# Attention in seven products: reordering the key loads, a third score half, the first denominators and the tail statistics

## The chip, the cores and the metric

The kernel runs on one core of one Trainium2 chip. The metric is the device time of one launch in microseconds, as the median of several runs. All times below are in microseconds unless they say otherwise. PE is TensorE's matmul row, PEld its weight loads, DVE is VectorE, ACT is ScalarE, POOL is GpSimd and SP is SyncE.

## What is computed

The input is four images of 256 channels and 64 x 64 positions, in fp32. The first layer is attention over all 4096 positions; the second is a block of cluster attention, an MLP and a pointwise convolution. Cut to what matters:

```
q = wq x + bq;  k = wk x + bk;  v = wv x + bv        # 32, 32 and 256 channels
attn = softmax(q^T k over all 4096 keys)
x = gamma * (v attn^T) + x                           # layer 0
y = x + ls1 * cluster(group_norm(x))                 # layer 1
y = y + ls2 * (W2 gelu(W1 group_norm(y)))
out = relu(bn(Wp relu(bn(y * dw))))
```

The group norm of layer 1 needs mean and variance over a whole image, so it can only begin when the attention of that image is complete.

## The kernel before

**Units.** `attention` (from L318) handles one image ("batch"). Its 4096 queries are eight blocks of 512 (`nb`), its keys eight groups of 512 (`g`). A unit `u = 8 nb + g` is one query block against one key group; there are 64 a batch. The 512 x 512 weights of a unit times the 512 x 256 values are done as a two by two block product with seven products in place of eight: `exps` (L591) subtracts the maxima (two L597 on DVE) and takes exponentials (L601 to L603 on ACT), `factors` (L608) makes the sums of quarters (L620 on DVE, four L606 on POOL), and `weigh` (L658) issues the 28 matmuls (L676) in four parts, 0 to 3, each part one or two of the seven products.

**Scores ahead of their use.** Scores are made up to eleven units ahead (`LEAD`), in halves: `half(u, h)` (L465) issues two matmuls of keys against queries (`products`, L433), ACT copies the result from PSUM into one of twelve slots (`kept`, L446), and DVE takes the elementwise maximum into `top` (L457). The two-buffer PSUM pool for scores has one buffer taken by the maxima (`hold`), so each half waits until the half before it has been released. Normally the release comes from DVE's maximum, which reads PSUM; a half marked `kept_only` is released by ACT's copy alone, and its maximum goes on the list `held`, to be taken from the slot later by `caught(n)`, in order of entry. The table `at` (from L865) spreads the halves over the units: two in a normal unit, ahead of parts 0 and 2 (`due`), and three, ahead of parts 0, 1 and 3, in the units listed in `three`, where they are `kept_only`.

**What else runs in a unit.** `weighting` (L888) writes the order of all engines by hand; `manual_schedule` keeps it, and each engine executes its own instructions in that order. In the order of a block:

- `begun(u)` (L413), with the first half of a unit, issues the load of the next unit's keys (`k_unit`, L411, 256 KB, on SP's queue; two key buffers).
- At `g = 1` and 2 of every block but the first, `total` (L724) reduces the block before to its denominators: DVE transposes and reduces (L544, L545), ACT copies (L551), DVE reduces again, takes the reciprocal (L735) and transposes (L561), then `rows` calls `everywhere` (L96), which writes a row of 512 values to DRAM (L99) and reads it back into all partitions (L100), both on SP's queue. The tile `few` that these steps write in is set to zero on POOL at its first use in a batch (L539).
- At `g = 5`, `highest` (L564) does the same for the maxima of the next block; `known` (L580, ACT) puts them into `hold` at `g = 6`. In block 0, transposes on PE do this instead (`short`).
- `gather` (L684) adds the partial denominators at `g = 7` (L692), on POOL, and on DVE in the last block.
- `evict` (ACT, L706) and `combined` (POOL, L717 to L722) turn the seven products' banks into the block's output; `leave` (POOL, L746) multiplies by the reciprocals and `sent` (two DMAs on SP's queue, L754) stores it.
- In the last units `tail` loads the input again (L106), adds the stored attention to it by DMA on POOL's queue (`back`, L770, and `back_one`, L775), and loads the weights that follow. `pooled` (L797) and `seen` (L792), both DVE, take cell sums and normalisation statistics of query blocks 0 to 5, one block per unit, as the table `views` says: units 57 to 62.

After unit 63 the last denominators are summed on PE (L1011) and inverted (L1020), the last block is finished on DVE (L721, L722, L1036, L788), its statistics are taken, and `group_norm` begins (L287, L289). PE is given filler meanwhile (`fill`): the value projection of the next batch (L388), or in batch 3 the last block of batch 2's MLP, which `mlp` leaves over for `late_block` (L1409). Its `begin` is called in unit 61 of batch 3: per channel half a copy of y on POOL (L1419) and a scaling on ACT (L1420), then a subtraction on POOL (L1429). `turn_mlp` (L230) forms two weight combinations on POOL (L233, L234), in batch 3 in the last `tail`.

Of the kernel before, what the change touches and what calls it, by code (L numbers as in the profile page):

```python
# [11 lines left out]
ALU = mybir.AluOpType  # L12
AX = mybir.AxisListType

P = 128
B, C, H, W = 4, 256, 64, 64
# [5 lines left out]
D = 32  # L22
# [38 lines left out]
def attention_then_cluster_block(  # L61
# [34 lines left out]
    def everywhere(dst, rows, name):  # L96

        d = dram.tile([NB], F32, tag="row", name=f"row_{name}")
        nc.sync.dma_start(out=d.rearrange("(a b) -> a b", b=D), in_=rows)  # L99
        nc.sync.dma_start(out=dst, in_=d.partition_broadcast(P))  # L100

    def load_x(b, t, dma=nc.sync):
        xb = x[b].rearrange("(k p) h w -> p k (h w)", p=P)
# [175 lines left out]
    def table(f):  # L279

        nc.scalar.activation(probe, probe, f)
# [36 lines left out]
    def attention(b, xs, ys):  # L318
# [240 lines left out]
        def rows(one, low, dst, name):  # L559

            nc.vector.transpose(low[:D, :D], one)  # L561
            everywhere(dst, low[:16, :D], name)

        def highest(nb):  # L564

            fold(nb)
            top = tops.pop(nb)
            low = spare()[:, nb % 2]
            steps = reduced(top[:, 0], top[:, 1], low, ALU.max, nc.scalar.copy)
            next(steps)  # L570
            yield
            next(steps)
            yield
            one = next(steps)
            mb = work.tile([P, NB], F32, tag="w2", bufs=1, name=f"mr_{b}_{nb}")
            rows(one, low, mb, f"mx_{b}_{nb}")
            yield mb

        def known(mb):
            nc.scalar.copy(own["hold"][:, 0], mb)  # L580
# [143 lines left out]
        def total(nb):  # L724

            few = spare()
            low = few[:, 2]
            flipped = few[:, 3:].rearrange("p a n -> p (a n)")
            steps = reduced(rdens[nb], flipped, low, ALU.add, nc.scalar.copy)
            next(steps)  # L730
            yield
            next(steps)
            yield
            one = next(steps)
            nc.vector.reciprocal(one[:, :16], one[:, :16])  # L735
            rows(one, low, rdens[nb], f"rd_{b}_{nb}")
            yield

        def over(nb):
# [127 lines left out]

        todo = [(p, h) for p in range(GRP + 1, units) for h in range(2)]
        for u in range(units):
            three = u in (1, 3, 9, 11)  # L870
            for part in (0, 1, 3) if three else (0, 2) if u else (1, 3):
                if todo:
                    p, h = todo.pop(0)
                    assert p <= u + LEAD
                    at[u, part] = p, h, three or not u
# [12 lines left out]
        def weighting(next_x, fill, early, begin):  # L888

            mb, av, den, peak, quarters = None, None, iter(()), iter(()), iter(())  # L890

            views = {units - 7 + i: i for i in range(6)}
            shifts = {units - 10: 0, units - 9: 1, units - 8: 2, units - 7: 3}

            def tail(u):


                for at_u, f in (
                    (units - 12, lambda: load(0)),
                    (units - 11, lambda: load(1)),  # L900
                    (units - 10, lambda: (load(2), back(0))),
                    (units - 9, lambda: (load(3), back(1))),
                    (units - 8, lambda: back(2)),
                    (units - 5, lambda: (next_x(), next_x())),
                    (units - 4, lambda: (load_mix(b), next_x())),
                    (units - 4, lambda: b == B - 1 and load_mlp(b)),
                    (units - 3, lambda: (next_x(), begin())),
                    (units - 2, lambda: b < B - 1 and load_mlp(b)),
                    (units - 1, lambda: b == B - 1 and turn_mlp()),
                ):  # L910
                    if u == at_u:
                        f()

            for u in range(units):
# [10 lines left out]
                        )  # L925
                    ]
                maxima = due(u, 0)
                if g == GRP - 1:
                    gather(nb)
                if g + 1 < GRP or more:  # L930
                    exps(u + 1)
# [2 lines left out]
                if nb < 2 or g == 6:  # L934
                    caught(1)

                if nb and g == 1:
                    den = total(nb - 1)
                    next(den)
                elif nb and g == 2:  # L940
                    next(den)
                elif ripe:
                    peak = highest(nb + 1)
                    next(peak)
                if early and nb > 1:
                    early.pop(0)()
                if u in views:
                    pooled(views[u])
                    seen(views[u], (0,))
                weigh(u, av, 0)  # L950
                if short:
                    two = ps_s.tile([P, 2, NB], F32, tag="s", name=f"tt_{b}_{nb + 1}")
# [29 lines left out]
                    spread(nb + 1, dgs["dg"])  # L982
                for f in due(u, 3):
                    f()
                if nb and g == 1:
                    next(den)
                elif nb and g == (4 if more else 3):
                    leave(nb - 1)
                elif nb and g == (5 if more else 4):
                    sent(nb - 1)  # L990
                weigh(u, av, 3)
                if g == 3 and nb + 2 < NBLK:
                    q_block(nb + 2)
# [10 lines left out]
            nb = NBLK - 1  # L1004
            for _ in range(4):
                next(quarters)
            table(AF.Sqrt)
            two = ps_s.tile([P, 2, NB], F32, tag="s", name=f"den_{b}_{nb}")
            den, inv = two[:, 0], two[:, 1]
# [399 lines left out]
    def late_block(b, y, gab):  # L1409
# [5 lines left out]
        def begin():  # L1415
            held["x"] = spool.tile([P, 2, KC, NB], F32, tag="s", name=f"xl_{b}")
            held["y"] = spool.tile([P, 2, KC, NB], F32, tag="s", name=f"yl_{b}")
            for k in range(KC):
                nc.gpsimd.tensor_copy(held["y"][:, 0, k], y[k])  # L1419
                nc.scalar.activation(  # L1420
                    held["x"][:, 0, k],
                    y[k],
# [3 lines left out]
                )  # L1426

            x = held["x"]
            nc.gpsimd.tensor_tensor(x[:, 1, 0], x[:, 0, 0], x[:, 0, 1], ALU.subtract)  # L1429

        def hidden(j):
            return held["h", j // 4][:, j % 4]
# [617 lines left out]
```

## Time and profile before

| | us |
|---|---|
| median of 3 runs (lowest to highest) | 3172.92 (3171.77 to 3178.33) |
| the profiled execution, its own time | 3181.04 |
| its span, first to last instruction | 3179.1 |
| PE busy, share | 3063.0, 96% |
| DVE busy, share | 2508.3, 79% |
| POOL busy, share | 2315.7, 73% |
| ACT busy, share | 1778.2, 56% |
| mean granted PE clock | 0.991 |

The 64 units of the four batches begin at 74.4, 860.4, 1637.9 and 2389.9 and end at 542.8, 1318.4, 2096.0 and 2860.5. In a line of the timeline the columns are start, duration, engine, line, operation, output and inputs with shapes, and in brackets how long the engine stood idle before it and what ended that. SPq is SP's instruction queue. In a line of waits the three numbers are the total, how often, and the longest. The profiler infers who ended a wait; matmul ends are modelled.

### The profile page before, as it was taken

The page shows a single profiled execution, that of the slowest core. Times are in us where ns is not written, and L with a number is a line of the kernel's source. Part 1 is how long each engine was busy: PE and PEld are TensorE (multiplying, and loading weights), DVE is VectorE, ACT ScalarE, POOL GpSimd, SP SyncE. Part 2 cuts the span into 40 slices and gives each one's busy share as a digit, 9 for nine tenths or more (in the row PEclk, how much of TensorE's full clock was granted, in tenths as well). Part 3 has the DMA queues.
Part 4 walks back from the last instruction along what each step waited for, and adds up shares of the span by engine and source line. Part 5 has one row for each costly group of instructions (what it writes and reads, how often), then busy time and mean ns, then how long its engine had stood idle before and what let it go on. Part 6 is the DMA issues. An engine that isn't in the chain of part 4 may idle for free.

```text
span 3179.1 us, 41316 instructions
## 1 busy us (share of the span) xinstructions
PE 3063.0 (96%) x14210; PEld 2503.5 (79%) x14210; DVE 2508.3 (79%) x3573; ACT 1778.2 (56%) x2815; POOL 2315.7 (73%) x2219
## 2 busy tenths in 40 slices
PE   7999999999999999999999999999999999998999
PEld 5777888788678888878867888886877788875786
DVE  3888888677788888877778888877768888876675
ACT  4656664545556666454455666644546566654444
POOL 3888888378578888647758888955767887893663
PEclk9999999999999999999999999999999999999999
DMA  5121126100111223510011212431011112150000
GB/s 165 40 63 60 54 64 190 67 20 27 46 48 59 61 62 98 153 57 27 18 57 44 67 60 64 119 128 44 27 40 50 57 50 67 54 151 1 14 21 27
DMA packets 105873, 200.39 MB, mean 63 GB/s; under 512 B 14416, under 2 KB 30400, under 8 KB 104128
## 3 DMA queue, kind: packets, MB, share of 16 engines
q1 hardware_dynamic: 101856, 181.94, 18.1%
q0 software_dynamic: 2976, 14.70, 2.4%
q8 instruction: 113, 1.85, 0.2%
q10 hardware_dynamic: 832, 1.11, 0.1%
q14 instruction: 96, 0.79, 0.1%
HBM read 149.37 MB, written 48.34 MB: 62 GB/s over the span
## 4 chain that ended last, share of the span: by engine, by line
PE 65%; POOL 13%; DVE 10%; DMA 5%; issue 3%; ACT 3%; SPq 0%; POOLq 0%; ACTq 0%; DVEq 0%
PE av L676 27%; PE mo L1662 9%; PE sc L433 6%; PE hq L1745 5%; POOL acc L606 4%; DMA k<-k 3%; PE hp L1745 3%; PE hr L1745 3%; PE fv L1234 3%; POOL t L606 3%; DVE top L457 2%; POOL s L606 2%; PE vp L388 2%; DVE s L597 2%; PE mo L1646 1%
## 5 line engine op out<-in xcount | busy, mean ns | idle before, releaser
L446 ACT COPY s<-sc 128x1024 f32<-128x1024 f32 x512 | 515.4, 1012 | 466.6 <-PE sc L433 455.4
L597 DVE TENSOR_TENSOR s<-s,hold 128x1024 f32<-128x1024 f32 x512 | 598.3, 1208 | 7.0 <-ACT hold L580 4.2
L606 POOL TENSOR_TENSOR acc<-acc,t 128x512 f32<-128x512 f32 x408 | 541.3, 1347 | 0.0
L606 POOL TENSOR_TENSOR s<-t,s 128x512 f32<-128x512 f32 x256 | 346.2, 1353 | 263.8 <-DVE t L620 197.0
L676 PE MATMUL av<-t,v 128*128 128x256 f32 x2048 | 530.3, 381 | 4.5 <-DVE t L620 2.4
L676 PE MATMUL av<-s,sum 128*128 128x256 f32 x2048 | 526.4, 379 | 4.5 <-POOL s L606 4.3
L676 PE MATMUL av<-s,v 128*128 128x256 f32 x2048 | 528.3, 381 | 2.1 <-ACT xn L1613 1.1
L457 DVE TENSOR_TENSOR top<-sc,top 128x1024 f32<-128x1024 f32 x350 | 426.6, 1219 | 47.1 <-ACT s L446 43.0
L620 DVE TENSOR_TENSOR t<-s,hold 128x1024 f32<-128x1024 f32 x256 | 311.3, 1216 | 191.4 <-POOL acc L606 82.2
L433 PE MATMUL sc<-q,k 128*128 128x512 f32 x1024 | 395.3, 471 | 58.5 <-DMA k<-k 27.0
L676 PEld LDWEIGHTS av<-t,v 128*128 128x128 f32 x2048 | 388.5, 191 | 69.2 <-DVE t L620 8.9
L676 PEld LDWEIGHTS av<-s,v 128*128 128x128 f32 x2048 | 389.1, 190 | 65.3 <-ACT xn L1613 2.3
L676 PEld LDWEIGHTS av<-s,sum 128*128 128x128 f32 x2048 | 388.4, 190 | 60.3 <-POOL s L606 7.6
L1700 ACT ACTIVATE hs<-hs,pv_s 128x256 f32<-128x256 f32 x496 | 232.7, 503 | 352.3 <-DVE hs L1736 352.3
L1662 PE MATMUL mo<-hs,w 128*128 128x256 f32 x1512 | 384.8, 381 | 0.0
L606 POOL TENSOR_TENSOR t<-s 128x512 f32<-128x512 f32 x256 | 329.7, 1288 | 54.5 <-PE av L676 41.2
L1662 PEld LDWEIGHTS mo<-hs,w 128*128 128x128 f32 x1512 | 283.8, 190 | 46.9 <-ACT hs L1700 6.2
L433 PEld LDWEIGHTS sc<-q,k 128*128 128x128 f32 x1024 | 175.6, 191 | 148.9 <-DVE top L457 68.4
L601 ACT ACTIVATE hold<-s 128x512 f32<-128x512 f32 x256 | 154.2, 602 | 224.4 <-DVE s L597 224.0
L603 ACT ACTIVATE s<-s 128x1024 f32<-128x1024 f32 x256 | 266.9, 1042 | 0.0
L1736 DVE TENSOR_TENSOR hs<-hq,hs 128x256 f32<-128x256 f32 x496 | 198.3, 420 | 86.0 <-PE hq L1745 76.0
L676 PE MATMUL av<-t,sum 128*128 128x256 f32 x1024 | 262.4, 378 | 0.0
(292 smaller groups left out, 4856.0 us busy)
## 6 DMA issues: line engine op xcount, KB each, us to landing
k<-k SPq DMA_DIRECT2D x256, 256.0 KB, 2.7
x<-in_x SPq DMA_DIRECT2D x62, 512.0 KB, 6.6
out<-xn SPq DMA_DIRECT2D x62, 256.0 KB, 2.1
att<-t SPq DMA_DIRECT2D x56, 256.0 KB, 3.8
x<-att POOLq DMA_DIRECT2D x12, 1024.0 KB, 9.7
q<-q SPq DMA_DIRECT2D x32, 256.0 KB, 4.1
w<-in_w SPq DMA_DIRECT2D x8, 1024.0 KB, 11.5
k<-hl_k SPq DMA_DIRECT2D x28, 256.0 KB, 2.6
```

The lines of the kernel that those rows point to most:

```text
L433: nc.tensor.matmul(sc[:, r, :], k_s[:, (2 * h + r) * P : (2 * h + r + 1) * P], qs[u // GRP], start=True, stop=True,)
L446: nc.scalar.copy(slots[u][:, PAIR[h]].rearrange("p h r n -> p r h n"), tiles(sc))
L457: nc.vector.tensor_tensor(top, src, top if saved[nb] is None else saved[nb], ALU.max)
L597: nc.vector.tensor_tensor(sh, sh, mb.to_broadcast([P, 2, 2, QW]), ALU.subtract)
L603: nc.scalar.activation(s[:, PAIR[1]], s[:, PAIR[1]], AF.Exp)
L606: nc.gpsimd.tensor_tensor(out, x, y, op)
L620: nc.vector.tensor_tensor(t31[u], s[:, B11 : B22 + 1 : 2], b12.to_broadcast([P, 2, 2, QW]), ALU.add)
L676: nc.tensor.matmul(av[bank][:, half_ * QW : (half_ + 1) * QW], a[:, r], t[:, r], start=(g == 0 and r == 0 and i in (1, 7, 2, 4)), stop=(g ...
L1662: return nc.tensor.matmul(bank[:, half * HB : (half + 1) * HB], a[:, j], t, start=start, stop=stop)
L1700: nc.scalar.activation(src, src, AF.Gelu_apprx_tanh, bias=pvc("b1", P, j + 4 * (i > 1)))
L1736: nc.vector.tensor_tensor(dst, ps, term, ALU.add)
L1745: nc.tensor.matmul(out, w, x, start=True, stop=True)
```

## The change

Seven edits, all in the order of work:

1. `everywhere` returns the reading of the row as a function instead of issuing it. `total` calls it at once. `highest` yields once more: the reading (L100) is issued at the beginning of `g = 6`, behind that unit's first half and so behind its key load, and `sent` of the block before follows it there (before, at the end of `g = 5`).
2. The units with three halves are 1, 3, 7 and 9 instead of 1, 3, 9 and 11.
3. In block 1, `total` begins at `g = 2` instead of `g = 1` and ends at `g = 3`.
4. A unit with three halves calls `caught(1)` once more, ahead of part 3.
5. `views` is a unit later (units 58 to 63), and `gather` of the last block comes behind that unit's first statistics instead of ahead of them.
6. `turn_mlp` in batch 3 comes behind the first four steps of the last `combined` instead of ahead of them.
7. In `late_block.begin`, the copies go from POOL to ACT and the subtraction from POOL to DVE.

```diff
         nc.sync.dma_start(out=d.rearrange("(a b) -> a b", b=D), in_=rows)
-        nc.sync.dma_start(out=dst, in_=d.partition_broadcast(P))
+        return lambda: nc.sync.dma_start(out=dst, in_=d.partition_broadcast(P))
...
             nc.vector.transpose(low[:D, :D], one)
-            everywhere(dst, low[:16, :D], name)
+            return everywhere(dst, low[:16, :D], name)
...
-            rows(one, low, mb, f"mx_{b}_{nb}")
+            fetch = rows(one, low, mb, f"mx_{b}_{nb}")
             yield mb
+            fetch()
+            yield
...
-            rows(one, low, rdens[nb], f"rd_{b}_{nb}")
+            rows(one, low, rdens[nb], f"rd_{b}_{nb}")()
...
-            three = u in (1, 3, 9, 11)
+            three = u in (1, 3, 7, 9)
...
-            views = {units - 7 + i: i for i in range(6)}
+            views = {units - 6 + i: i for i in range(6)}
...
-                    (units - 1, lambda: b == B - 1 and turn_mlp()),
...
                 maxima = due(u, 0)
-                if g == GRP - 1:
+                if more and nb and g == GRP - 2:
+                    next(peak)
+                    sent(nb - 1)
+                if g == GRP - 1 and more:
                     gather(nb)
...
-                if nb and g == 1:
+                when = 1 if nb > 1 else 2
+                if nb and g == when:
                     den = total(nb - 1)
                     next(den)
-                elif nb and g == 2:
+                elif nb and g == when + 1:
                     next(den)
...
                     seen(views[u], (0,))
+                if g == GRP - 1 and not more:
+                    gather(nb)
                 weigh(u, av, 0)
...
-                if nb and g == 1:
+                if nb and g == when:
                     next(den)
                 elif nb and g == (4 if more else 3):
                     leave(nb - 1)
-                elif nb and g == (5 if more else 4):
+                elif nb and g == 4 and not more:
                     sent(nb - 1)
+                if (u, 0) in at and (u, 1) in at:
+                    caught(1)
                 weigh(u, av, 3)
...
             for _ in range(4):
                 next(quarters)
+            if b == B - 1:
+                turn_mlp()
...
-                nc.gpsimd.tensor_copy(held["y"][:, 0, k], y[k])
+                nc.scalar.copy(held["y"][:, 0, k], y[k])
...
-            nc.gpsimd.tensor_tensor(x[:, 1, 0], x[:, 0, 0], x[:, 0, 1], ALU.subtract)
+            nc.vector.tensor_tensor(x[:, 1, 0], x[:, 0, 0], x[:, 0, 1], ALU.subtract)
```

## The prediction

> **What bounds the kernel now.** I read the page's engine line and its chain first.
>
> ```profile
> PE 3063.0 (96%) x14210; PEld 2503.5 (79%) x14210; DVE 2508.3 (79%) x3573; ACT 1778.2 (56%) x2815; POOL 2315.7 (73%) x2219
> ...
> PE 65%; POOL 13%; DVE 10%; DMA 5%; issue 3%; ACT 3%; SPq 0%; POOLq 0%; ACTq 0%; DVEq 0%
> ```
>
> TensorE (PE) sets the time; an edit pays only where PE stands still. Next, busy time by stretch: query blocks 1, 2 and 7 of batch 1, then block 7 of batch 3 (blocks begin at their first L676 matmul).
>
> ```profile
> 923.10:986.30 63.20, 58.60 (x261) 48.45 (x260) 53.81 (x52) 38.65 (x56) 54.49 (x43) 1.00 0.19 59
> 986.30:1043.00 56.70, 56.51 (x258) 47.91 (x257) 50.06 (x50) 37.11 (x54) 49.25 (x42) 1.00 0.20 61
> 1266.30:1318.40 52.10, 50.60 (x225) 41.70 (x224) 45.66 (x49) 24.98 (x37) 50.94 (x45) 1.00 0.83 223
> 2805.20:2860.50 55.30, 50.55 (x225) 41.66 (x223) 44.65 (x49) 26.32 (x39) 54.42 (x48) 1.00 0.63 146
> ```
>
> Columns are length, then PE, PEld, DVE, ACT, POOL busy. Block 2 is the steady state: 8 units of 7.0 us. Counting from first matmul to first matmul of a unit, a unit with no score half lasts 6.04, so a half costs 0.48. Block 1 is 6.5 longer than block 2, of which 2 x 0.48 are extra halves. In block 7 PE waits because POOL works 50.94 of 52.10: **there POOL is the bound**. Third, PE's waits:
>
> ```profile
> PE sc L433 <- DMA k<-k: 27.0, 25, 2.2
> PE sc L433 <- DVE top L457: 16.7, 22, 2.0
> PE sc L433 <- ACT s L446: 9.5, 33, 1.5
> ```
>
> Fourth, the timeline at the longest key wait (batch 0, block 3, end of g = 6):
>
> ```profile
> 305.72 0.32 SPq L99 DMA_DIRECT2D row_mx<-few  x1
> ...
> 308.94 0.32 SPq L100 DMA_DIRECT2D mr<-row_mx  x1
> ...
> 309.31 0.94 SPq L754 DMA_DIRECT2D att<-t  x2
> ...
> 310.34 11.09 SPq L411 DMA_DIRECT2D k<-k  x3
> ...
> 311.35 1.22 DVE L457 TENSOR_TENSOR top<-sc,top 128x1024 f32<-128x1024 f32 x1
> ...
> 314.77 0.69 PE L433 MATMUL sc<-q,k 128*128 128x512 f32 x2 [2.18 <-DMA k<-k]
> ```
>
> The key load stands behind a read that waits for the row's write to land. The score bank was free at 312.57; the keys were 2.2 late. Fifth, where block 1 loses:
>
> ```profile
> 936.07 0.43 POOL L539 MEMSET few<- 128x384 f32 x1
> ...
> 936.53 0.69 DVE L545 TENSOR_REDUCE few<-few 128x16 f32<-128x512 f32 x1 [2.40 <-POOL few L539]
> ...
> 942.93 0.72 PE L433 MATMUL sc<-q,k 128*128 128x512 f32 x2 [1.26 <-DVE top L457]
> ...
> 950.85 0.70 PE L433 MATMUL sc<-q,k 128*128 128x512 f32 x2 [1.15 <-DMA k<-k]
> ```
>
> In unit 9, which has three halves, VectorE (DVE) also begins the first denominators and stands 2.40 for a memset queued on POOL; score banks then come free late. Sixth, the end of batch 3:
>
> ```profile
> 2851.10 1.63 POOL L1419 COPY yl<-y 128x512 f32<-128x512 f32 x2
> ...
> 2852.70 1.70 POOL L1429 TENSOR_TENSOR xl<-xl 128x512 f32<-128x512 f32 x1
> ...
> 2856.78 1.13 PE L676 MATMUL av<-s,sum 128*128 128x256 f32 x4 [3.33 <-POOL s L606]
> ...
> 2864.34 0.69 DVE L721 TENSOR_TENSOR t<-t,t 128x512 f32<-128x512 f32 x1 [1.94 <-POOL t L720]
> ```
>
> [...] half-clock windows of 3.41 us follow key waits at 315.5, 2510.3 and 2687.8. [...]
>
> **The change, part by part.** Times are differences to the profiled execution; minus is a gain.
>
> *Keys first.* After L99 the queue now holds k (issue 0.32, landing 2.7 median), then L100, then two att (0.94 together). Key waits at the end of g = 6 are 6.5, 1.2, 1.7 and 7.5 in the four batches: -16.9. The rest of the 27.0 lies in block 1's g = 3 (5.6, counted below), before the first units and in the opening. k is now issued 0.4 after L99, lands about 3 to 4.5 after it, and is wanted 6.5 to 9 after: no wait is left. Next late is the row of maxima, landed 3.5 after L100. L100 waits for L99's landing (1.3, or 2.6 to 3.1 in seven blocks) either way, so the row moves by at most a few tenths. In the seven slow blocks L580 already waited 7.9 in all; PE, coming sooner, meets that by about 0.2 each: +1.5. The three half-clock windows go, each worth half of 3.41: -5.1. `sent` only follows; its reader is units away. In block 6 no keys follow; there two x loads (0.43 issue each, 4.05 and 4.90 to landing at 1247.6) now stand ahead of L100, and the row comes 0.5 to 1.5 later on ACT's queue, with the shift and exps behind it. POOL has 2.0 of slack there: I take +0.3 a batch, +1.2 (0 to +6).
>
> *Three halves in units 7, 9 instead of 9, 11, and denominators at g = 2, 3.* Worked with 1.0 per ACT copy, 1.13 per maximum, 2.26 per pair of subtractions, 2.1 per exps, 1.26 per POOL sum. Unit 7: ACT's three copies, exps and four evictions (2.2) need 7.5; 7.9. Unit 8: DVE starts its subtractions 1.3 late; 7.95. Unit 9: 7.9, like units 1 and 3 (7.93), as no reduction stands in it. Unit 10: POOL's sums and L719/L720 come before the memset, so the reduction still waits about 0.7 and delays both maxima; 8.35. Units 11 and 12: 7.0. Sum 46.1, against 48.9 now: -2.8 a batch, -11.2 (0 to -18). The denominators' DMAs, a unit later, end three or more units before a key is wanted; `leave` at g = 4 finds them landed with about 0.5 to spare.
>
> *The extra `caught(1)`.* A maximum moves from unit 4 into unit 3, ahead of unit 4's subtractions, and waits there for the third copy: +0.3 a batch, +1.2 (-1 to +3).
>
> *Tail statistics a unit later.* Unit 57 loses 2.6 of DVE work, where batch 1 waited 1.2 for x<-att. But POOL stands only 0.3 between 1262 and 1320, and block 7 lasts 52.0 to 52.1 in three batches though their stalls differ; PE's end stays. In unit 63 the reduction (1.13) and one statistic (0.60) now come before `gather`, whose sum feeds the last denominators. It waited 0.56 for POOL in batches 0 and 2, 0 in batch 1; add 0.05 for the other statistic: +1.2, +1.8, +1.2 = +4.1 (-4 to +8). PE's longer idle can bring a half-clock window: +0.5.
>
> *Batch 3's work off POOL.* Two copies and the subtraction were 3.33 on a saturated queue. ACT takes two copies of 0.6 to 0.75 where it stands idle. DVE waits about 0.6 for ACT and subtracts (0.67 as L690 alone, 1.75 as L690 beside POOL; I take 0.67), ahead of unit 63's subtractions, so t comes 1.3 later: PE gains 2.4, not 3.3. `turn_mlp` (3.1) behind L717 to L720 frees L721: 1.94, less 0.5 for the statistics: -1.4. Then PE need not stand 2.66 before the group norm, after which the clock fell to half for 6.83 us and the norm took 7.6 against 4.2 in batch 1: -3.0 (0 to -3.4).
>
> **Sum:** -16.9 + 1.5 - 5.1 + 1.2 - 11.2 + 1.2 + 4.1 + 0.5 - 2.4 - 1.4 - 3.0 = **-31.5**, from the profiled execution's 3181.0 (its span of 3179.1 and 1.9 around it): 3149.5. The median of the runs is 3172.9, 8.1 less. If that is a constant the new median is 3141.4; if it is the slow rows and half clocks of this one execution, which the change makes harmless, it is 3149.5. I lean to the latter: **3148**.
>
> **Rivals.** (1) *Block 1 keeps its stalls*: ACT is full in unit 7, evictions late, the memset still last in unit 10; the 11.2 vanish: about 3160. For: ACT at 7.5 of 7.5. Against: unit 11 has nothing left in it. (2) *The row of maxima takes the keys' place*: behind k's 256 KB it lands later by 1.5 or more, L580 holds ACT, and the 16.9 and 5.1 come down to about 4: 3167. For: L580 has no slack in slow blocks. Against: k has mostly landed when L100 is issued. (3) *The tail turns slower*, the case on the other side: statistics hold back the denominators, [...] and the fill work (some 8 us) runs at half clock in every batch, as in the 13.65 us at 2940. Price: 2.6 + 6.8 a batch, 37.6 where I put 4.6 and with batch 3's 3.0 lost too: +4.5 on 3181, near 3180 for the median. It decides from about 8.5 a batch. [...] (4) *POOL's bound gives way* once no statistic waits for x<-att: block 7 nears 8 x 6.04, 3 us a batch and the 4.6 gone: about 3132.
>
> **How the numbers follow.** Forecast 0.57 (3140 to 3156), rival 1 0.16, rival 2 0.10, rival 3 0.06, rival 4 0.11. The range 3136 to 3166 holds the first two and the nearer parts of rivals 2 and 4. Measurement tells about 0.2% (6.3 us, 3166.6): faster 0.87; same 0.07, from rival 2's upper half and failures together; slower 0.06.
>
> **What would show it.** Right: key waits on PE under 10 us; g = 6 near 7.2; units 7 to 12 near 46; block 7 of batch 3 near 53; the final denominators 1 to 2 later after block 7 in batches 0 to 2; fewer half-clock windows. Wrong: L580 waiting over 15 us in all; a half-clock window after unit 63 in every batch; unit 10 still above 9.5.

## The result and the profile after

| | before | after |
|---|---|---|
| median of 18 runs each, side by side | 3172.0 | 3166.06 |
| lowest to highest | 3164.9 to 3181.14 | 3160.92 to 3170.23 |
| ratio, 95% interval | | 0.9981 (0.9973 to 0.9989) |
| the profiled execution, its own time | 3181.04 | 3166.07 |
| its span, mean granted clock | 3179.1, 0.991 | 3164.3, 0.993 |

The change makes the kernel 0.19% faster, 5.9 us by the medians and 15.0 between the two profiled executions, where 3148 was forecast: faster, but by about a quarter of the 24.9 by which the forecast lay below 3172.9. The page of the kernel after, the engine line and the chain's shares:

```profile
PE 3058.6 (97%) x14210; PEld 2499.2 (79%) x14210; DVE 2510.8 (79%) x3574; ACT 1779.7 (56%) x2817; POOL 2321.1 (73%) x2216
...
PE 68%; POOL 14%; DVE 10%; issue 3%; DMA 2%; ACT 2%; SPq 0%; POOLq 0%; ACTq 0%; DVEq 0%
```

PE's share of the chain rose from 65 to 68%, DMA's fell from 5 to 2%; DVE's 10% stayed. That is the first hint: the waits for DMA are gone, those for VectorE are not. PE's waits in the kernel after say the same (total, how often, longest). Lines up to L561 keep their numbers, later ones stand two to eleven further down: the copy of the maxima is L582 (was L580), the subtractions are L599 (was L597), the sums L622 and L608 (were L620 and L606), the matmuls of the units L678 (was L676).

```profile
PE sc L433 <- DVE top L457: 27.9, 45, 2.4
PE sc L433 <- ACT s L446: 9.5, 32, 1.5
...
PE sc L433 <- DMA k<-k: 5.0, 4, 3.0
```

Key waits fell from 27.0 to 5.0, as forecast (under 10). Waits for VectorE's maxima rose from 16.7 to 27.9, where the forecast wanted them to fall. Block 1 of batch 1 and block 7 of batch 3 by stretch (length, then PE, PEld, DVE, ACT, POOL busy):

```profile
924.02:986.46 62.44, 58.19 (x259) 48.09 (x258) 53.62 (x52) 37.59 (x54) 54.35 (x44) 1.00 0.20 60
...
2797.59:2849.50 51.91, 50.20 (x224) 41.92 (x224) 45.20 (x49) 27.58 (x41) 50.25 (x44) 1.00 0.64 153
```

Block 7 of batch 3 came down from 55.3 to 51.9. Block 1 only went from 63.2 to 62.4, although one of its extra score halves (0.48) moved into block 0: PE still stands 4.25 us in it. Unit by unit (first matmul to first matmul), batch 1:

| unit | 2 | 4 | 5 | 7 | 8 | 9 | 10 | 11 | 12 | 7 to 12 |
|---|---|---|---|---|---|---|---|---|---|---|
| before | 7.16 | 7.28 | 7.39 | 7.01 | 7.00 | 8.00 | 9.75 | 9.32 | 7.82 | 48.9 |
| forecast | | | | 7.9 | 7.95 | 7.9 | 8.35 | 7.0 | 7.0 | 46.1 |
| after | 7.99 | 8.17 | 7.01 | 8.05 | 8.36 | 7.94 | 10.29 | 7.00 | 7.00 | 48.6 |

Nearly all of the forecast's gain in units 7 to 12 is missing in two places, unit 10 (1.9 late) and unit 8 (0.4). Units 2 and 4, for which 0.3 together had been put, lost 0.8 and 0.9, and unit 5 got 0.4 back. The timeline of the kernel after shows unit 10:

```profile
944.88 0.69 DVE L544 STREAM_TRANSPOSE few<-rden 128x512 f32<-128x512 f32 x1
...
946.59 0.42 POOL L539 MEMSET few<- 128x384 f32 x1
947.04 0.69 DVE L545 TENSOR_REDUCE few<-few 128x16 f32<-128x512 f32 x1 [1.47 <-POOL few L539]
...
950.04 0.73 PE L433 MATMUL sc<-q,k 128*128 128x512 f32 x2 [1.71 <-DVE top L457]
```

The reduction of the first denominators still waits for the memset of its tile, which stands on POOL behind the sums and L721 and L722. The score halves wait behind that on VectorE. The theory I took from this: **block 1 is held up by the memset, and edit 4's extra catch adds a second delay**; the keys, the tail and batch 3 went as forecast. The rivals: the key edit brings next to nothing in most executions (its local gain seemed to be 1.1 a batch, given back in block 6); or VectorE has too much to do in blocks 0 and 1, whatever the order.

### The profile page after: what moved, and what is told of

It reads as the page before. It is cut to its first block, busy times and chain, and to the rows that moved or that the text cites. A ratio compares the mean times of both kernels' runs of the same rounds, so it can differ in the third digit from the quotient of the medians.

```text
span 3164.3 us, 41331 instructions
## 1 busy us (share of the span) xinstructions
PE 3058.6 (97%) x14210; PEld 2499.2 (79%) x14210; DVE 2510.8 (79%) x3574; ACT 1779.7 (56%) x2817; POOL 2321.1 (73%) x2216
## 4 chain that ended last, share of the span: by engine, by line
PE 68%; POOL 14%; DVE 10%; issue 3%; DMA 2%; ACT 2%; SPq 0%; POOLq 0%; ACTq 0%; DVEq 0%
PE av L678 29%; PE mo L1673 10%; PE sc L433 6%; POOL acc L608 5%; PE hq L1756 5%; PE hp L1756 3%; POOL t L608 3%; PE hr L1756 3%; PE fv L1245 3%; POOL s L608 2%; DVE top L457 2%; PE vp L388 2%; DVE s L599 1%; PE mo L1657 1%; DVE t L622 1%
## 5 line engine op out<-in xcount | busy, mean ns | idle before, releaser
L599 DVE TENSOR_TENSOR s<-s,hold 128x1024 f32<-128x1024 f32 x512 | 598.7, 1209 | 12.4 <-ACT hold L582 10.3
L608 POOL TENSOR_TENSOR acc<-acc,t 128x512 f32<-128x512 f32 x408 | 536.2, 1334 | 0.0
L678 PE MATMUL av<-s,v 128*128 128x256 f32 x2048 | 526.1, 379 | 6.6 <-ACT t L708 4.0
L678 PE MATMUL av<-s,sum 128*128 128x256 f32 x2048 | 526.8, 380 | 3.6 <-POOL s L608 3.4
L678 PE MATMUL av<-t,v 128*128 128x256 f32 x2048 | 526.8, 380 | 1.8 <-POOL t L608 1.8
L608 POOL TENSOR_TENSOR s<-t,s 128x512 f32<-128x512 f32 x256 | 339.7, 1327 | 251.5 <-DVE t L622 184.7
L622 DVE TENSOR_TENSOR t<-s,hold 128x1024 f32<-128x1024 f32 x256 | 312.0, 1219 | 205.3 <-POOL acc L608 108.7
L678 PEld LDWEIGHTS av<-s,v 128*128 128x128 f32 x2048 | 386.9, 189 | 70.3 <-ACT t L708 5.6
L433 PE MATMUL sc<-q,k 128*128 128x512 f32 x1024 | 395.1, 470 | 47.6 <-DVE top L457 27.9
L457 DVE TENSOR_TENSOR top<-sc,top 128x1024 f32<-128x1024 f32 x350 | 426.6, 1219 | 14.4 <-ACT s L446 10.4
L678 PEld LDWEIGHTS av<-t,v 128*128 128x128 f32 x2048 | 387.7, 190 | 61.5 <-POOL t L608 6.5
L678 PEld LDWEIGHTS av<-s,sum 128*128 128x128 f32 x2048 | 388.1, 190 | 60.9 <-POOL s L608 8.4
L608 POOL TENSOR_TENSOR t<-s 128x512 f32<-128x512 f32 x256 | 340.6, 1331 | 47.1 <-PE av L678 34.1
L678 PE MATMUL av<-t,sum 128*128 128x256 f32 x1024 | 262.4, 378 | 0.0
## 6 DMA issues: line engine op xcount, KB each, us to landing
x<-in_x SPq DMA_DIRECT2D x62, 512.0 KB, 5.6
```

The costliest lines, as they stand in the source:

```text
L433: nc.tensor.matmul(sc[:, r, :], k_s[:, (2 * h + r) * P : (2 * h + r + 1) * P], qs[u // GRP], start=True, stop=True,)
L457: nc.vector.tensor_tensor(top, src, top if saved[nb] is None else saved[nb], ALU.max)
L599: nc.vector.tensor_tensor(sh, sh, mb.to_broadcast([P, 2, 2, QW]), ALU.subtract)
L608: nc.gpsimd.tensor_tensor(out, x, y, op)
L622: nc.vector.tensor_tensor(t31[u], s[:, B11 : B22 + 1 : 2], b12.to_broadcast([P, 2, 2, QW]), ALU.add)
L678: nc.tensor.matmul(av[bank][:, half_ * QW : (half_ + 1) * QW], a[:, r], t[:, r], start=(g == 0 and r == 0 and i in (1, 7, 2, 4)), stop=(g ...
```

## The experiments

Twelve kernels ran in three groups of four (e1 to e4, e5 to e8, e9 to e12), each group on another chip and beside the kernel before, whose medians were 3177.66, 3173.39 and 3172.41; so a time is best read through its ratio. Where kernels of different groups are compared, neither reading is safe: the kernel before took 4 to 5 longer in the first group than in the others, but e4 there and e5 in the second group agree within 0.5 in blocks 0 to 5. The ratios may then make too much of e1 to e4. Each of them was also profiled. This table sums stretches over the four batches, from the profiles (us): units 0 to 6, units 7 to 12, blocks 0 and 1 (units 0 to 15), blocks 2 to 5, blocks 6 and 7, and the time from the end of unit 63 to the group norm's first matmul. "Threes" are the units with three halves.

| kernel | median | ratio to before (95%) | 0-6 | 7-12 | blocks 0, 1 | 2 to 5 | 6, 7 | to norm |
|---|---|---|---|---|---|---|---|---|
| before | 3172.0 | 1 | 224.1 | 195.4 | 510.7 | 922.4 | 422.1 | 41.0 |
| after | 3166.06 | 0.9981 (0.9973-0.9989) | 230.4 | 194.6 | 512.2 | 908.9 | 421.5 | 42.5 |
| e1, keys alone | 3161.57 | 0.9958 (0.9943-0.9973) | 224.1 | 193.5 | 504.4 | 910.0 | 426.2 | 39.0 |
| e2, threes alone | 3176.58 | 0.9998 (0.9988-1.0007) | 224.3 | 196.0 | 510.7 | 921.5 | 423.9 | 40.8 |
| e3, no extra catch | 3163.6 | 0.9958 (0.9944-0.9972) | 224.1 | 197.7 | 508.7 | 911.1 | 421.8 | 42.5 |
| e4, row first in block 6 | 3165.15 | 0.9966 (0.9953-0.9979) | 233.0 | 194.6 | 514.7 | 908.5 | 419.4 | 42.5 |
| e5, changed again | 3166.45 | 0.9979 (0.997-0.9988) | 233.0 | 194.7 | 514.8 | 908.9 | 421.6 | 42.5 |
| e6, early memset | 3161.98 | 0.9963 (0.995-0.9977) | 230.8 | 188.9 | 507.0 | 908.7 | 422.0 | 42.5 |
| e7, early memset, no catch | 3145.22 | 0.9912 (0.99-0.9925) | 224.3 | 180.6 | 491.8 | 909.0 | 421.5 | 42.5 |
| e8, tail undone | 3162.76 | 0.9967 (0.9954-0.998) | 230.5 | 194.7 | 512.0 | 909.0 | 421.7 | 41.0 |
| e9, memset alone | 3165.91 | 0.9975 (0.9964-0.9985) | 224.2 | 186.6 | 501.2 | 918.0 | 423.9 | 40.4 |
| e10, old thirds | 3151.93 | 0.9925 (0.9913-0.9938) | 224.3 | 185.4 | 495.3 | 909.7 | 421.7 | 42.5 |
| e11, batch 3 off POOL | 3168.69 | 0.9989 (0.9981-0.9996) | 224.1 | 193.3 | 508.6 | 920.7 | 422.3 | 40.8 |
| e12, mended | 3142.73 | 0.9904 (0.9888-0.9919) | 224.2 | 180.5 | 491.1 | 909.4 | 420.9 | 40.8 |

**Keys alone.** The kernel before with edit 1.

```diff
-        nc.sync.dma_start(out=dst, in_=d.partition_broadcast(P))
+        return lambda: nc.sync.dma_start(out=dst, in_=d.partition_broadcast(P))
...
+            fetch()
+            yield
...
+                if more and nb and g == GRP - 2:
+                    next(peak)
+                    sent(nb - 1)
...
-                elif nb and g == (5 if more else 4):
+                elif nb and g == 4 and not more:
```

> The kernel before with edit 1 alone (keys ahead of the reading of the row, `sent` behind it). Theory A (local gains as the changed kernel's trace shows them): blocks 2 to 5 gain about 1.1 a batch, unit 55 loses 1.0 to 1.7 (7.0 or more instead of 6.04) because two x loads now stand ahead of the reading of the row, so that an undisturbed batch gains nothing; what is left is the rare slow row: median 0 to 6 us below the kernel before. Theory B (the prediction's sum, lost elsewhere): key waits were worth 16.9 and half-clock windows 5.1 in every execution: median 15 to 22 below. In both the key waits on PE fall below 6 in all.

It came out 16.1 below by the medians, about 13 by the ratio. My theory A fell and the prediction's own sum (19.3 for these terms) came near: blocks 2 to 5 gave 12.4, blocks 0 and 1 gave 6.3, and key waits on PE went from 27.0 to 9.3 (not under 6: 4.3 is left in block 1 and the rest outside the units). Block 6 lost about 1.0 to 1.6 a batch, and block 7 gave 0.6 of it back. The key edit by itself is faster than the whole change by its ratio, though the intervals touch: edits 2 to 7 together brought nothing, or cost some us.

**Threes and denominators alone.** The kernel before with edits 2 and 3.

```diff
-            three = u in (1, 3, 9, 11)
+            three = u in (1, 3, 7, 9)
...
-                if nb and g == 1:
+                when = 1 if nb > 1 else 2
+                if nb and g == when:
...
-                elif nb and g == 2:
+                elif nb and g == when + 1:
```

> The kernel before with edits 2 and 3 alone (three halves in units 1, 3, 7, 9; first denominators at g = 2 and 3), without the extra catch. Theory A: unit 7 takes 8.0 and unit 10 still 9.5 to 10.3, because the reduction still waits over 1 us for the memset queued on POOL; units 7 to 12 stay at 48 to 49.5 as before, the median within 3 us of the kernel before. Theory B: it is the extra catch in unit 9 that delays unit 10; without it unit 10 takes about 8.4 and units 7 to 12 take 46 to 47: median 8 to 12 below.

Theory A: 1.1 below, ratio 0.9998, unit 10 at 10.4 to 10.9 without any extra catch, units 7 to 12 unchanged. The wait for the memset is 2.4 in each batch, as in the kernel before. The term of 11.2 was not there to be had by these two edits.

**No extra catch.**

```diff
-                if (u, 0) in at and (u, 1) in at:
-                    caught(1)
```

> The changed kernel without edit 4 (the extra catch ahead of part 3). Theory A: units 2 and 4 go back to about 7.2 and 7.3 (8.0 and 8.2 with it), unit 5 to 7.4; 1.0 to 1.4 a batch, and more in batch 0: 4 to 7 us below the changed kernel. Theory B: the held maxima only pile up and are paid later, in units 8 to 12 or at the fold: no difference, or up to 4 slower.

Units 2 and 4 went back to 7.2 and 7.3 (8.1 and 7.3 in batch 0) as theory A says (units 0 to 6: 6.3 less than in the changed kernel), and unit 8 to 7.06. But units 7 to 12 took 3.1 more, so theory B is half right: part is paid again in units 10 and 11. The sum is 2.9 below the rerun of the changed kernel by the medians and some 7 by the ratios, across groups; by the spans of the profiles it is 2.3 and 3.5 below the two executions of the changed kernel, so I take about 3. The timeline shows why so little came of it. Changed kernel, where unit 3's third half is caught ahead of unit 4's subtractions:

```profile
888.51 1.22 DVE L622 TENSOR_TENSOR t<-s,hold 128x1024 f32<-128x1024 f32 x1 [0.64 <-issue]
...
891.95 1.23 DVE L457 TENSOR_TENSOR top<-s,top 128x1024 f32<-128x1024 f32 x1 [1.08 <-ACT s L446]
...
893.09 2.35 DVE L599 TENSOR_TENSOR s<-s,hold 128x1024 f32<-128x1024 f32 x2
```

The same place without the catch:

```profile
885.78 1.22 DVE L622 TENSOR_TENSOR t<-s,hold 128x1024 f32<-128x1024 f32 x1 [0.63 <-issue]
...
888.05 2.34 DVE L599 TENSOR_TENSOR s<-s,hold 128x1024 f32<-128x1024 f32 x2
```

From L622 to the subtractions it is 4.58 with the catch and 2.27 without: the 1.08 for ACT's third copy and 1.23 for the maximum lie on VectorE ahead of everything that unit 4 needs. And this is unit 10 without the catch:

```profile
939.57 0.70 DVE L544 STREAM_TRANSPOSE few<-rden 128x512 f32<-128x512 f32 x1
...
942.20 0.42 POOL L539 MEMSET few<- 128x384 f32 x1
942.66 0.69 DVE L545 TENSOR_REDUCE few<-few 128x16 f32<-128x512 f32 x1 [2.39 <-POOL few L539]
...
945.67 0.79 PE L433 MATMUL sc<-q,k 128*128 128x512 f32 x2 [3.21 <-DVE top L457]
```

VectorE, no longer late, arrives earlier at the reduction and waits the longer for the memset: 2.39 instead of 1.47, and PE stands 3.21. With the catch PE stood 1.71. The two delays lay side by side: without the catch, the wait for the memset lasts longer.

**The row first in block 6.** In block 6 no keys follow, so the reading of the maxima can go straight behind their writing there.

```diff
                     mb = next(peak)
+                    if nb == NBLK - 2:
+                        next(peak)
...
-                    next(peak)
+                    if nb < NBLK - 2:
+                        next(peak)
```

> The changed kernel, but in block 6, where no keys follow, the row of maxima is read at once behind its writing, as before, and so ahead of the two x loads. Theory A: unit 55 goes back from 7.0 or 7.7 to 6.04 to 6.2, the waits of PE for the evictions (av <- t) from 4.0 to under 1 in all: 4 to 6 us below the changed kernel. Theory B: block 7 is bound by POOL, so the time only moves into block 7 (51.4 becomes 52.1): under 1.5 below in all.

Blocks 6 and 7 together fell by 2.2 in the four batches, the medians by 1.3 across groups (some 4 by the ratios, whose intervals overlap): by the profiles it is between the two theories, nearer to B. The changed kernel's timeline at this place in batch 1:

```profile
1253.79 0.32 SPq L99 DMA_DIRECT2D row_mx<-few  x1
1254.22 0.84 SPq L106 DMA_DIRECT2D x<-in_x  x2
1255.16 0.37 SPq L100 DMA_DIRECT2D mr<-row_mx  x1
...
1260.74 0.59 ACT L582 COPY hold<-mr 128x512 f32<-128x512 f32 x1 [2.54 <-DMA mr<-row_mx]
```

The reading follows its x loads and lands 5.5 after it is issued, where it takes 3.3 to 4.2 in the blocks before. Unit 55 takes 7.0 to 7.7 for it; with the reading first it takes 6.04 in batches 0 and 2, 6.6 to 6.8 in the others. But block 7, bound by POOL, then lasts 52.0 to 52.1 in batches 0 and 2 instead of 51.5: a third of the loss (1.1 of 3.3) was no loss.

**The changed kernel again**, unchanged, beside the next three.

> The changed kernel itself, beside the runs of the kernel before on the same chip, to set its parts against it. The key edit alone was 16.1 us faster by the medians, and its profile differs from the changed kernel's by 1.3 to 2.7 a batch in blocks 0 and 1 (the changed one slower) and by 4.6 in batch 3's block 7 (faster). Theory A (edits 2 to 4 cost in net, 5 to 7 bring less than that): 9 to 14 us below the kernel before. Theory B (edits 2 to 7 are worth nothing in sum): 15 to 17 below.

It was 6.9 below, less than theory A's 9 to 14. The first group's 16.1 for the keys alone and 6.9 here are not of one group; by ratios the gap is 0.2%, with 0.9958 (0.9943-0.9973) against 0.9979 (0.997-0.9988). The profiles put it in blocks 0 and 1, 504.4 for the keys alone, 512.2 and 514.8 in two executions of the changed kernel, and in the time to the norm (39.0 against 42.5); in blocks 6 and 7 the changed kernel is 4.6 to 4.7 faster.

**Early memset.** One line at the end of unit 4 of every batch; `spare` makes the tile and sets it to zero where it is first called.

```diff
+                if u == 4:
+                    spare()
```

> The changed kernel with one step moved: the tile of the reductions is set to zero on POOL at the end of unit 4 of each batch, not at its first use in unit 10. Theory A (the memset, queued last on POOL, is the wait that ends last in unit 10): VectorE's wait of 1.47 goes and unit 10 comes down from 10.3 to 8.6 to 9.0, units 7 to 12 from 48.6 to 47: 5 to 7 us below the changed kernel. Theory B (unit 10 is late since VectorE begins it 1.15 late and has over 7 us of work in it): unit 10 stays above 9.9, under 2 us in all.

Theory A: unit 10 went from 10.30 to 8.85, by nearly the whole 1.47, and units 7 to 12 from 48.67 to 47.22; the median is 4.5 below the changed kernel in the same group, though the intervals of the two ratios overlap.

**Early memset and no catch.** Both edits just shown.

> The changed kernel with the memset at the end of unit 4 and without the extra catch of edit 4. Theory A (memset and catch are two separate causes; without them the prediction's term for units 7 to 12 holds): unit 8 takes 7.06, unit 10 7.5 to 8.4, unit 11 7.0 to 7.5, units 7 to 12 together 45 to 46.2, and units 2 and 4 go back to 7.2 and 7.3: 12 to 17 us below the changed kernel. Theory B (VectorE has too much to do in blocks 0 and 1, and what is taken out of one unit comes back in the next): units 7 to 12 stay above 47.5, at most 6 below.

3145.22, which is 21.2 below the changed kernel in the same group; one edit alone gave 4.5, the other about 3. Units 7 to 12 took 45.15 and unit 10 8.09. Theory A, and more than it asked for: 12 to 17 had been expected. Its timeline in unit 10:

```profile
930.02 0.70 DVE L544 STREAM_TRANSPOSE few<-rden 128x512 f32<-128x512 f32 x1
930.75 0.69 DVE L545 TENSOR_REDUCE few<-few 128x16 f32<-128x512 f32 x1
...
933.76 0.73 PE L433 MATMUL sc<-q,k 128*128 128x512 f32 x2 [0.85 <-DVE top L457]
```

No wait stands in the bracket of the reduction, and PE stands 0.85 instead of 3.21. In blocks 0 and 1 the catch undone and the early memset save 3.5 and 5.2 apart and 20.4 together of the changed kernel's 512.2 (6.1, 7.8 and 23.0 of the rerun's 514.8). Seen from the other side, each of the two is worth 15 to 17 there once the other is out of the way. This rules out the rival that VectorE has too much to do there: in blocks 0 and 1 of batch 1 it was busy for 110.4 of 122.5, against 109.6 of 127.6 in the changed kernel.

**The tail undone.**

```diff
-            views = {units - 6 + i: i for i in range(6)}
+            views = {units - 7 + i: i for i in range(6)}
...
-                if g == GRP - 1 and more:
+                if g == GRP - 1:
                     gather(nb)
...
-                if g == GRP - 1 and not more:
-                    gather(nb)
```

> The changed kernel with edit 5 taken back (statistics and cell sums from unit 57 on, `gather` ahead of them). Theory A (as predicted: POOL binds block 7, so edit 5 gains nothing there and holds back the last denominators): end of the units to group norm falls from 10.43 to 9.5 to 9.9 in batches 0 to 2, block 7 stays within 0.1 of 51.44: 1 to 4 us below the changed kernel. Theory B (edit 5 is what lets block 7 end 0.6 earlier): block 7 goes back to 52.05, 1 to 3 above.

Theory A in direction: end of units to group norm 10.14, 10.38, 9.46 and 10.97 instead of 10.42, 10.42, 10.43 and 11.18, together 1.5; block 7 within 0.03 in batches 0 to 2. Edit 5 costs about 1.5 in the profile (3.7 by the medians of one group, whose ratio intervals overlap) and gains nothing. The table says the same: 42.5 to the norm in all seven kernels with edit 5, 39.0 to 41.0 in the seven without it.

**The memset alone**, in the kernel before (the same two lines).

> The kernel before with nothing but the memset moved to the end of unit 4 of each batch. Theory A (the memset alone, not where the three halves stand, made block 1 late): VectorE's wait of 2.40 in unit 9 goes, units 7 to 12 fall from 48.9 to 45.5 to 46.5: 9 to 13 us below the kernel before. Theory B (edits 2 and 3 are needed as well: the reduction shares unit 9 with three halves): units 7 to 12 stay at 47 to 48.5, 2 to 7 below.

Units 7 to 12 fell to 46.6, just short of theory A's figure, and the time by 6.5 (ratio 0.9975), within theory B's. The memset alone takes 9.5 out of blocks 0 and 1, and moving this one step brings as much as the seven edits did.

**Old thirds.** The kernel of e7 with edits 2 and 3 taken back.

```diff
-            three = u in (1, 3, 7, 9)
+            three = u in (1, 3, 9, 11)
...
-                when = 1 if nb > 1 else 2
-                if nb and g == when:
+                if nb and g == 1:
...
-                elif nb and g == when + 1:
+                elif nb and g == 2:
```

> The kernel of the last run but two (changed, memset early, no extra catch; 3145.2 us, units 7 to 12 45.15) with edits 2 and 3 taken back: three halves in units 9 and 11 again, first denominators at g = 1 and 2. Theory A (edits 2 and 3 are worth little once the memset is out of the way): units 7 to 12 take 45.5 to 46.3, 2 to 5 us above that kernel. Theory B (they were worth the better part of the 14 a batch group gained): 47 or more, 8 to 13 above.

6.7 above e7 by the medians of two groups, between the theories; units 7 to 12 take 46.6 in three batches and 45.5 in one, against 45.15. Edits 2 and 3 are thus worth 4.8 in the profile once the memset and the catch are out of the way, not 11.2. What is left with the old order is unit 11, 9.4 long, where a key load stands behind the denominators' row:

```profile
940.72 0.70 PE L433 MATMUL sc<-q,k 128*128 128x512 f32 x2 [1.28 <-DMA k<-k]
```

**Batch 3 off POOL.** The kernel before with edits 6 and 7.

```diff
-                nc.gpsimd.tensor_copy(held["y"][:, 0, k], y[k])
+                nc.scalar.copy(held["y"][:, 0, k], y[k])
...
-            nc.gpsimd.tensor_tensor(x[:, 1, 0], x[:, 0, 0], x[:, 0, 1], ALU.subtract)
+            nc.vector.tensor_tensor(x[:, 1, 0], x[:, 0, 0], x[:, 0, 1], ALU.subtract)
...
-                    (units - 1, lambda: b == B - 1 and turn_mlp()),
...
+            if b == B - 1:
+                turn_mlp()
```

> The kernel before with edits 6 and 7 alone (batch 3: copies to ACT, subtraction to VectorE, the weight combinations behind the first four steps of the last output). Theory A (the prediction's terms, 2.4 + 1.4 + up to 3.0, as the changed kernel's profile bears out): block 7 of batch 3 falls from 55.3 or 56.5 to 52.0 to 53.5, the last denominators of batch 3 come 0 to 1.4 sooner: 3 to 7 us below the kernel before. Theory B (POOL, freed in block 7, only stands and the end moves by less): block 7 stays above 54, under 2 in all.

3.7 below (0.9981 to 0.9996): the time is theory A's, the place theory B's. Block 7 of batch 3 took 55.6 in the profiled execution. The wait of 3.33 for POOL is gone, but others stand in its place:

```profile
2843.42 1.56 DVE L1430 TENSOR_TENSOR xl<-xl 128x512 f32<-128x512 f32 x1 [0.57 <-ACT xl L1421]
...
2850.80 1.89 PE L676 MATMUL av<-t,v 128*128 128x256 f32 x4 [1.13 <-DVE t L620]
```

The subtraction, now on VectorE ahead of unit 63's subtractions, took 1.56 (1.04 in the kernel after, 0.67 forecast), PE stood 0.57 for ACT and 1.13 for VectorE, and for 3.41 from 2851.0 on the granted clock was 0.50, within unit 63. In the profile the end of the batch gained, 1.0 to the group norm and 3.4 behind it, where the clock no longer fell. The 3.4 isn't shown to be these edits' doing. From the group norm to the next step on PE it is 4.2 in eight of the ten executions with edits 6 and 7 and 5.9 in two (e6 and e7); without them it is 7.6 in the kernel before, 5.9 in e1 and e9, and 4.2 in e2. What they do to block 7 is seen where the keys go first too: 56.5 in e1 without them, 52.1 in e8 with them.

**Mended.** The changed kernel with the four corrections: early memset, no catch, edit 5 undone, the row first in block 6.

> The changed kernel with what the runs showed to cost put right: memset at the end of unit 4, no extra catch, edit 5 taken back, and in block 6 the row of maxima read ahead of the x loads. Theory A (the four are independent of each other): 1 to 4 us below the kernel with the first two alone (3145.2), so 3141 to 3144; end of units to group norm 9.5 to 10.4, unit 55 6.04 to 6.8. Theory B (POOL and the norm take it back): within 1 of it.

3142.73, the best of all: 0.96% below the kernel before. Beyond e7 it is 2.5 by the medians, but the ratio intervals overlap (0.9888-0.9919 and 0.99-0.9925), so the last two corrections are shown by their stretches only: 1.7 to the norm and 0.6 in blocks 6 and 7, where batch 3's block 7 (53.35 instead of 51.96) gave back a good part of what the other batches gained: PE stands 0.57 and 1.13 at the same two places as in e11.

## Why the prediction failed, step by step

In short: the keys and batch 3 brought about what was forecast. The reordering of block 1 brought nothing, since a memset that moved along kept VectorE waiting, and since a maximum that was pulled forward made VectorE late.

Predicted terms against the profiles (us over four batches, minus is a gain):

| step | predicted | measured | from |
|---|---|---|---|
| keys first, rows, half clock | -20.5 | -18.7 | e1 less before: -12.4 in blocks 2 to 5, -6.3 in blocks 0 and 1 |
| block 6, x loads ahead of the row | +1.2 | about +2 | e5 less e4, blocks 6 and 7 |
| threes and first denominators | -11.2 | +4.2 | e3 less e1, units 7 to 12 |
| extra catch | +1.2 | +3.5 | after less e3, blocks 0 and 1 (+6.1 with e5 for after) |
| tail statistics | +4.6 | +1.5 | after less e8, end to norm |
| batch 3 | -6.8 | -7.1 | after less before: block 7 -3.4, to the norm -0.3, behind it -3.4 (the clock, not shown to be the edits', see e11) |
| sum | -31.5 | -14.6 | spans: -14.8 |

**The step that failed** is the one on units 7 to 12, and in it the sentence "Unit 10: POOL's sums and L719/L720 come before the memset, so the reduction still waits about 0.7 and delays both maxima; 8.35". The queue was right, the size of the wait was not, and the prediction shows no working for its 0.7. The waits of VectorE give it for the kernel before (total, how often, longest):

```profile
DVE few L545 <- POOL few L539: 9.6, 4, 2.4
```

It reads the same in e2 and e3, where the reduction comes a unit later, and 5.9, 4, 1.5 in the kernel after. Moving the reduction moved the memset with it, as it is made at the tile's first use, behind the sums of its new unit; so the wait stayed at 2.4, and it is 1.5 in the kernel after only because the extra catch makes VectorE late there. Unit 10 is its length without the wait, plus the wait: 8.09 (e7) and 2.39 make 10.48, where it is 10.4 to 10.9 in e3; 8.85 (e6) and 1.47 make 10.32, where the kernel after has 10.3. The forecast's 8.35 has 0.7 of wait in it. The memset was also most of what there was to gain: its early place alone (e9) shortens units 7 to 12 by 8.8, where 11.2 had been put down to edits 2 and 3. Rival 1 named it ("the memset still last in unit 10; the 11.2 vanish") and got 0.16; its 3160 was also too low, since the catch came on top.

**The second miss** is the extra catch. I priced it at one maximum less one maximum moved and a small wait, +0.3 a batch. It cost 6.3 in units 0 to 6 and returned 3.1 in units 7 to 12 (the kernel after less e3). The catch was placed ahead of the subtractions of the next unit, which start the chain to PE (subtractions, exponentials, sums, matmuls), while the work that it spared VectorE later was not due for units.

**The two hide each other.** The late start of VectorE in unit 10 (the catch) and the late memset both end at the same reduction. Taking the catch away lengthens the wait for the memset, from 1.47 to 2.39, and unit 11 behind it takes 8.7 to 9.3 instead of 7.0; taking the memset away gives back its 1.47 and leaves what the catch costs. So neither undoing alone came near the forecast, and both together came to it: 3145.2 against 3148, units 7 to 12 at 45.15 against 46.1, unit 10 at 8.09 against 8.35. That speaks for the rest of the sum, though e7 is not the kernel that was forecast: its wait is 0, not 0.7, and its tail lost less than was put.

**What held.** Key waits, block 7 of batch 3 (51.9; 53 forecast), block 7 bound by POOL (busy for 50.25 of 51.91 in batch 3), and a tail that got slower, by a third of what I put. The 3.0 for the clock behind batch 3's last unit came between these two executions, but less of it in e6 and e7. Two small slips stand in the sum: 1.2 + 1.8 + 1.2 is 4.2, not 4.1, and 3.3 less 1.3 is 2.0, not 2.4. Rivals 2 and 4 did not come: blocks 2 to 5 lie at 56.5 to 57.0 nearly everywhere, batch 0's block 2 apart (59.5), and block 7 at 51.4, not 8 x 6.04. That rival 2's number, 3167, lies 1 from the measured time is chance: it wanted the worth of the key edit lost, and e1 shows that it came. Nor did rival 3: from the norm to the next step on PE it is 4.2 in all four batches of the kernel after.

**A sign that misled.** I had written that L580 waiting over 15 us would show the key edit wrong. In the kernel after the same copy waits 19.6 for the row, as the waits of ACT show,

```profile
ACT hold L582 <- DMA mr<-row_mx: 19.6, 11, 3.2
```

and the key edit was right all the same. Of the 19.6, 10.8 are the four waits of block 6, which I had priced apart, and 8.8 the seven in blocks with slow rows (2.4 or more from the issue of the writing to its landing), where it was 7.9 before. The four of those seven blocks that have no other stall last 56.6 to 57.0: the wait is ACT's, which has slack there, and PE hardly sees it. A sign should be tied to the stretch and to the engine that it is about.

**Profile and median.** I leaned to the new median being the profile's sum, not 8.1 below it. That held: the changed kernel's profiled execution (3166.07) is its median (3166.06). Of my reason, one half fell. The slow rows are not of one execution: in all fourteen profiled executions 11 or 12 of the 52 row writes took 2.4 us or more to land (1.3 is the median), at the same places, blocks 1 to 4 of batch 3 and 1 to 3 of batch 0 among them. The half clocks do differ. The half-clock windows add up to 58 in that execution, to 43 in the profile of the kernel after and to 34 in that of e1; half of 58 is 0.9% of the span, which is its mean granted clock of 0.991. The runs of the kernel before beside e1, e5 and e11 had medians of 0.993, 0.994 and 0.993, and among them a thousandth of clock went with 1.2 to 1.9 us. By that, as an estimate, 2 to 5 of the 8.1 go with the clock; the rest stays open, and so does what is cause there, since windows also follow waits: ahead of each of the three of 3.41 that the prediction names PE stood for 2.0 to 2.2, ahead of the 6.83 behind batch 3's last unit for 2.66, and ahead of the 13.65 at 2940 for 3.44. That the waits bring the windows, on which the forecast's 5.1, 0.5 and 3.0 rest, was my estimate and is not shown. A gain that is summed from a high execution is partly a gain over that execution only, which is why 15.0 between profiles is 5.9 between medians.

**What stays open.** Why the catch costs batch 0 2.4 to 4.6 in blocks 0 and 1 and the others 1.1 at most (unit 2 there takes 10.1 to 11.6, and 8.1 without it) stays open, and so does why just those row writes are slow. Whether the keys alone beat the whole change by 0.2% rests on two groups and their profiles.

## What to carry to other kernels

When a step is moved, find every instruction that is created at its first use and moves with it, here a memset of 0.42 us behind the sums of a unit on a busy queue; a one-time preparation belongs well ahead of its use, where nothing waits for it. When two delays end at one instruction, removing either shows only a small part of its price, so test them together before calling either harmless: here 4.5, about 3, and 21.2 us. Work that is pulled forward on an engine is only free if it does not stand ahead of the head of a chain that ends at the bound engine: here a maximum of 1.23 and its wait of 1.08 stood there, and units 0 to 6 took 6.3 longer in the four batches.

## What was not expected of the hardware

The maxima of halves marked `kept_only` have a dearer form, with the extra catch (median 1.32, up to 2.35, in the kernel after) or without it (median 1.39, up to 2.37, in the kernel before), where those taken from PSUM have a median of 1.22. The instructions of L457 in the kernel after (ns, lowest, median, highest):

```profile
L457 DVE TENSOR_TENSOR top<-sc,top x350: 1204/1218/1226, 37.9 to 2777.1; 128x1024 f32<-128x1024 f32 x175
L457 DVE TENSOR_TENSOR top<-s,top x56: 1218/1324/2353, 81.9 to 2470.4; 128x1024 f32<-128x1024 f32 x56
```

A maximum whose scores are still in PSUM (sc) never took more than 1.23 us; one caught later from the slot in SBUF (s) took up to 2.35. The trace also shows what the excess is. The 12 of the 56 that began while POOL stood took 1.22. The 44 that began beside a running POOL instruction ended 1.08 after it, or after their own 1.22 if that was later: with 0.63 of it left they took 1.71, with 1.02 left 2.10, with 1.08 left 2.17. Of the 350 maxima from PSUM 223 began beside one too, and none took over 1.23. Releasing a score bank early by `kept_only` has that price here, up to 1.13 (2.35 less 1.22), on top of the wait for ACT's copy (1.08 ahead of unit 4). And a small write to DRAM that another transfer waits for is not of one duration: 1.3 us for most rows, and 2.4 to 6.5 for 11 or 12 of 52, the longest of them (over 3.9) in block 7 of each batch, where x and the attention are being loaded; it varied with the place in the program far more than from one execution to the next.
